# A graph network's merged stage: project the next group in the steps that attend to this one

## The chip, the cores and the metric

The kernel runs on one core of one Trainium2 chip. A core has a TensorE (PE, matmuls into PSUM), a VectorE (DVE), a ScalarE (ACT), a GpSimd (POOL) and a SyncE (SP, which here only issues DMAs). Each engine works through its own list of instructions in order and waits on semaphores for the others. The metric is the device time of one execution in microseconds; less is better.

## The reference

Two layers over 32768 nodes of 256 numbers and 524288 edges. Cut to what matters:

```python
h = relu(layernorm(x))                      # layer 0: attention within 128 nodes
Q, K, V = h @ Wq + bq, h @ Wk + bk, h @ Wv + bv     # 256 blocks, 8 heads of 32
scores = Q @ K.T / sqrt(32)                 # block 0 also adds a bias made of its edges
x = x + softmax(scores) @ V @ Wo + bo
h = relu(layernorm(x))                      # layer 1: one step of a gated graph network
h = (h - mean) * rsqrt(var + EPS) * gamma + beta    # over all nodes
a_in  = segment_sum((h @ W_in + b_in)[src] * iw, dst)
a_out = segment_sum((h @ W_out + b_out)[dst] * ow, src)
x = x + gated_update(h, [a_in, a_out] @ W_x2i + b_x2i, h @ W_h2h)
```

## The kernel before

The program has these stages in order: sort and count the edges and write tables (to about 950 us), attention of the first group, the merged stage (to about 9970 us), the sums over edges (to about 17100 us), and the gated update.

**Groups.** The attention is cut into 64 groups of 512 nodes, four blocks `b` of 128 each. `group(g)` (L719) gives the whole work of one group as a table from a step number to functions: `@at(t)` files a function under step `t`. Its parts, with their steps: load x into `xg` on ACT's queue (L744, step 0), add the bias row to it on POOL into `xb` (L748, step 3), layer norm (`row_stats`, `std`, reciprocal, `xn`: steps 2 to 8), transposes into `hT` (L739, L779: 6 to 10), queries and keys for the two halves `m` of the heads (L789, L795: 11 to 18; copied out at L799 and L808/L810), values (L820: 19 to 23). Then for each block `b`, from step B = 17 + 11 b: for each half `m`, scores (L837, at B + 4 m), their maximum (L845), exps on ACT (L851, two to a step), transposes of the exps (L857, from B + 3 and B + 7), their copy (L863/L865); then the product with the values (L873, B + 10 and 11), division (L880), transpose (L739, B + 13), output matmul (L895), sum with `xb` and statistics (L899, B + 16). After blocks 2 and 3: the root (`std`, L734), norm (L922), transposes (L739) and copies of the new rows, and their writes to memory. The last step is 71.

Queries lie in `qT`; keys in `kbd`, a tile with zeros between the heads; there is one set of each. The matmuls of a group write three PSUM banks, `mm`, `pt` and `sc`, one buffer each: a bank's next user waits until the one before is copied out.

**The merged stage.** `spread(k, lo, hi)` works for each of three parts of the edges in rounds of CI = 64 steps, 68 rounds in all. Each step handles a set of 128 edges, in a chain of operations that stand some steps apart (`steps`, L1115):

```python
steps = ((0, fetch), (4, spread_lanes), (6, select), (8, rank), (8, product), (8, place), (9, scale), (9, scatter))
```

`fetch` loads 128 rows `hb` (SP, ring of 10 buffers); `rank` is three bf16 matmuls into `R` (PE, two banks); `product` a float32 matmul into `mp` (PE, two buffers); `place` reads `R` (DVE, `jk`); `scale` copies `mp` into a message (ACT); `scatter` sends four messages each fourth step by an indirect DMA (POOL). `window` and `derive` prepare the next round's tables from step 10 and 24 on.

`turns` (L1117) writes the loop: a body of four rounds (`UG`) or of one, in which the steps are written out by hand in order for PE, DVE, ACT and SP (`manual_schedule`; POOL isn't in it). Within a step come the edge operations first, then the group's functions of that step. A round that carries a group adds the table of `group(g)` to its steps (L1130 to 1133); what lies past step 63 falls into the next round's first steps or, at the end of a body, into eight steps that only drain. At the end of a body all engines meet, and the loop starts empty.

The edges read rows that the groups write, so the groups must run ahead: the first group is done by `alone` (L950) before the stage, and a loop at L960 does more if a count made from the tables says so. 63 of the 68 rounds carry a group, in 21 loop bodies, 14 of four rounds and 7 of one; the last five rounds carry none.

Of the kernel before, what the change touches and what calls it, by code (L numbers as in the profile page):

```python
# [11 lines left out]
F32 = mybir.dt.float32  # L12
# [487 lines left out]
def gnn_kernel(ctx, tc, x, src, dst, edge_attr, edge_type, w_in_e, w_out_e,  # L500
# [186 lines left out]
    with ExitStack() as c1:  # L687
# [10 lines left out]
        kbd = ap.tile([P, KC, GB, HC, P], F32, name="kbd")  # L698
        nc.gpsimd.memset(kbd, 0.0)
# [14 lines left out]
        hT, qT, h1T = (ap.tile([P, KC, GN], F32, name=n) for n in ("hT", "qT", "h1T"))  # L714
# [4 lines left out]
        def group(g, bias=None):  # L719
# [3 lines left out]
            def at(t):  # L723
                def put(f):
                    todo.setdefault(t, []).append(f)
                return put

            def row_stats(i, b, rows):
                st = ab.tile([P, 6], F32, name="st")
                nc.vector.bn_stats(st, rows)  # L730
                nc.vector.bn_aggr(mv[i][:, b], st)

            def std(i, bs):
                nc.scalar.activation(rstd[i][:, bs], mv[i][:, bs, 1], AF.Sqrt, bias=eps)  # L734

            def transposed(name, rows):
                tp = a_ps.tile([P, KC, P], F32, name=name)
                for k in range(KC):
                    nc.tensor.transpose(tp[:, k], rows[:, k * P:(k + 1) * P], ident)  # L739
                return tp  # L740

            @at(0)
            def _():
                nc.scalar.dma_start(xg, x_g[g])  # L744

            @at(3)
            def _():
                nc.gpsimd.tensor_add(xb, xg, bo_b[:, None, :].to_broadcast([P, GB, D]))  # L748

            for b in range(GB):  # L750
# [3 lines left out]
                @at(2 + b // 2)  # L754
                def _(b=b):
                    row_stats(0, b, xg[:, b])

                if b == 0:
                    @at(4)
                    def _():  # L760
                        std(0, slice(0, GB))

                    @at(5)
                    def _():
                        nc.vector.reciprocal(rstd[0], rstd[0])

                @at(5 + b)
# [5 lines left out]
                @at(6 + b)  # L773
                def _(b=b, row=row):
                    row["tp"] = transposed("pt" if b % 2 else "mm", row["xn"])

                @at(7 + b)
                def _(row=row, cols=cols):
                    nc.scalar.activation(hT[:, :, cols], row["tp"], AF.Relu)  # L779

            for m in range(KC):
                ps = {}
                mc = slice(m * P, (m + 1) * P)
                for k in range(KC):
                    @at(11 + 4 * m + k)
                    def _(m=m, k=k, ps=ps, mc=mc):
                        if k == 0:
                            ps["q"] = a_ps.tile([P, GN], F32, name="mm")
                        nc.tensor.matmul(ps["q"], wq[:, k, mc], hT[:, k], start=(k == 0), stop=(k == KC - 1))  # L789

                    @at(13 + 4 * m + k)
                    def _(m=m, k=k, ps=ps, mc=mc):
                        if k == 0:
                            ps["k"] = a_ps.tile([P, GN], F32, name="pt")
                        nc.tensor.matmul(ps["k"], wk[:, k, mc], hT[:, k], start=(k == 0), stop=(k == KC - 1))  # L795

                @at(13 + 4 * m)
# [3 lines left out]
                for j in range(HC):  # L801
                    @at(15 + 4 * m + j // 2)
# [9 lines left out]
            for b in range(0, GB, 2):  # L812
                ps = {}
                for i in range(2):
                    @at(19 + 3 * (b // 2) + i)
                    def _(b=b, i=i, ps=ps):
                        if i == 0:
                            ps["v"] = a_ps.tile([P, 2, D], F32, name="mm")
# [4 lines left out]
                @at(21 + 3 * (b // 2))  # L823
                def _(b=b, ps=ps):
                    nc.scalar.copy(vg[:, b:b + 2, :, 0:DH], ps["v"].rearrange("p b (h d) -> p b h d", d=DH))

            for b in range(GB):
                B = 17 + 11 * b
# [88 lines left out]
                for n, u in enumerate(range(bs.start, bs.stop)):  # L917
                    h = {}

                    @at(B + 18 + n)  # L920
# [3 lines left out]
                    @at(B + 19 + n)  # L924
                    def _(u=u, h=h):
                        h["tp"] = transposed("pt" if u == 1 else "sc", h1g[:, u])
# [497 lines left out]
```

## Time and profile before

| | us |
|---|---|
| median of seven runs | 19516.0 (19507.79 to 19544.12) |
| the profiled execution | 19532.19 |
| its span, first to last instruction | 19530.4 |
| PE busy | 14804.8 (76%) |
| DVE busy | 10004.3 (51%) |
| POOL busy | 9288.9 (48%) |
| ACT busy | 6698.5 (34%) |
| granted PE clock, mean | 0.885 |

Busy times are of the whole span and mix four stages, so they don't say what sets a stage's time. "A <- B" in a line means that A stood idle until B ended, with the total, the number of times and the longest. "issue" as a releaser means that nothing visible was waited for, and "remote" a release from outside the core's engines. The granted clock is the share of PE's full clock that it was given.

### The profile page before, as it was taken

The numbers are of one execution on the slowest core, as the hardware profiler recorded it, in microseconds if no ns is written. First come the engines' busy times: TensorE is split into PE (matmuls) and PEld (weight loads), VectorE is DVE, ScalarE is ACT, GpSimd is POOL, SyncE is SP. The second block draws the span as 40 slices with busy tenths as digits, with TensorE's granted clock in tenths as the row PEclk, the third lists the DMA queues.
The fourth block names the chain that finished last, engine by engine and source line by source line (L and its number), as shares of the span: only waits on it lengthen the run. The fifth ranks groups of instructions, "written<-read, shape, count | busy, mean of one in ns | idle before, by whom it ended". The sixth has DMA issues, their size and how long they took to land. (4 is left out here: it accounts for less than half of the span.)

```text
span 19530.4 us, 292322 instructions
## 1 busy us (share of the span) xinstructions
PE 14804.8 (76%) x71746; PEld 10613.8 (54%) x71746; DVE 10004.3 (51%) x33799; ACT 6698.5 (34%) x16865; POOL 9288.9 (48%) x9307
## 2 busy tenths in 40 slices
PE   2078777787777777777668787778787778788889
PEld 2055555555555455555456666666666666653334
DVE  8666666566666566665444444444444444432222
ACT  0044444444444444444223333333333333320000
POOL 0045545455554455544555555555555555532222
PEclk6598889888888898988779999899998998999999
DMA  2044444444444444444446666677766677673332
GB/s 64 7 146 151 147 144 148 135 147 148 147 145 143 138 129 145 147 142 140 134 143 196 193 197 196 183 199 198 196 197 184 193 197 199 195 151 111 108 111 96
DMA packets 1829625, 2975.41 MB, mean 152 GB/s; under 512 B 299498, under 2 KB 1288135, under 8 KB 1827670
## 3 DMA queue, kind: packets, MB, share of 16 engines
q1 hardware_dynamic: 1169398, 1550.90, 26.3%
q0 software_dynamic: 430768, 1160.40, 20.3%
q10 hardware_dynamic: 227888, 246.51, 4.0%
q8 instruction: 577, 9.45, 0.2%
q14 instruction: 994, 8.14, 0.1%
HBM read 2123.63 MB, written 1248.64 MB: 173 GB/s over the span
## 5 line engine op out<-in xcount | busy, mean ns | idle before, releaser
L1108 POOL DMA_INDIRECT msg_d<-msg,pi x4352 | 4287.3, 985 | 3962.6 <-issue 1719.8
L1230 POOL DMA_INDIRECT rows<-h_d,ixc x3584 | 3398.8, 948 | 2323.6 <-issue 744.0
L1099 DVE SCALAR_TENSOR_TENSOR jk<-iota,edc,R 128x256 f32<-128x256 bf16 x4352 | 2077.1, 478 | 3064.6 <-PE R L1079 1443.8
L1091 ACT ACTIVATE msg<-mp,edc 128x256 f32<-128x256 f32 x4352 | 2048.6, 476 | 3614.2 <-PE mp L1075 1893.6
L1265 ACT ACTIVATE selo<-lane_row,sl 128x128 f32<-128x128 f32 x5040 | 1661.3, 391 | 4696.3 <-DVE sl L1262 1596.9
L1244 PE MATMUL ps_i<-rows,sel 128*128 128x257 f32 x8960 | 2637.0, 415 | 811.2 <-DVE acc L1248 415.8
L1272 PE MATMUL ps_o<-m,selo 128*128 128x257 f32 x10080 | 2754.0, 413 | 587.1 <-ACT selo L1266 265.0
L1075 PE MATMUL mp<-hb,selT 128*128 128x256 f32 x8704 | 2875.5, 415 | 131.2 <-issue 74.0
L1272 PEld LDWEIGHTS ps_o<-m,selo 128*128 128x128 f32 x10080 | 1969.3, 205 | 981.9 <-issue 289.4
L1244 PEld LDWEIGHTS ps_i<-rows,sel 128*128 128x128 f32 x8960 | 1641.1, 207 | 1106.6 <-DVE acc L1248 476.7
L1237 DVE TENSOR_SCALAR sel<-lane_row,ed 128x128 f32<-128x128 f32 x4480 | 1393.6, 360 | 1006.1 <-PE idle L1245 378.4
L1079 PE MATMUL R<-oh,ones_b 128*128 128x256 bf16 x4352 | 1275.4, 293 | 500.9 <-DVE jk L1099 268.5
L1276 DVE SCALAR_TENSOR_TENSOR acc<-acc,blk,ps_o 128x257 f32<-128x257 f32 x1680 | 806.2, 480 | 1553.8 <-PE ps_o L1272 569.9
L1075 PEld LDWEIGHTS mp<-hb,selT 128*128 128x128 f32 x8704 | 1453.0, 210 | 268.2 <-issue 99.9
L1071 DVE TENSOR_SCALAR oh<-iota,edc 128x256 bf16<-128x256 bf16 x4352 | 1356.9, 312 | 4.1
L1079 PE MATMUL R<-oh,tri 128*128 128x256 bf16 x4352 | 1269.9, 292 | 0.0
L1079 PE MATMUL R<-oh,triu 128*128 128x256 bf16 x4352 | 1266.8, 292 | 2.6 <-DVE jk L1099 2.5
L1248 DVE SCALAR_TENSOR_TENSOR acc<-acc,blk,ps_i 128x257 f32<-128x257 f32 x2240 | 1071.1, 478 | 249.8 <-issue 69.6
L1230 POOL DMA_INDIRECT rows<-h_d,ixh x896 | 849.7, 948 | 649.9 <-issue 252.6
L1262 DVE TENSOR_SCALAR sl<-m,blk 128x3 f32<-128x3 f32 x1680 | 419.6, 250 | 1248.3 <-DMA m<-msg_d 1043.5
L1266 ACT ACTIVATE selo<-selo,one 128x384 f32<-128x384 f32 x1680 | 1031.3, 614 | 52.2
L1245 PE MATMUL idle<-lane_row,sel 128*128 128x128 f32 x4480 | 869.6, 283 | 166.8 <-DVE sel L1237 136.4
(366 smaller groups left out, 20442.0 us busy)
## 6 DMA issues: line engine op xcount, KB each, us to landing
m<-msg_d SPq DMA_DIRECT2D x1680, 396.0 KB
hb<-h_d SPq DMA_DIRECT2D x4352, 128.0 KB
sin_d<-acc SPq DMA_DIRECT2D x2240, 128.5 KB
sout_d<-acc SPq DMA_DIRECT2D x1680, 128.5 KB
msg_d<-msg,pi POOLq DMA_INDIRECT x4352
more<-sout_d ACTq DMA_DIRECT2D x128, 514.0 KB
rows<-h_d,ixc POOLq DMA_INDIRECT x3584
a<-sin_d ACTq DMA_DIRECT2D x64, 514.0 KB
```

The costliest lines, as they stand in the source:

```text
L1071: nc.vector.tensor_scalar(oh, cn["iota1"], c["ed"][:, 0, q:q + 1], None, op0=ALU.is_equal)
L1075: nc.tensor.matmul(mp, turn["sel", i // 4][:, q % 4], turn.pop(("hb", i)), start=True, stop=True)
L1079: nc.tensor.matmul(R[to % 2], cn[what], oh, start=False, stop=False, skip_group_check=True)
L1091: nc.scalar.activation(msg[:, q % 4, 0:D], turn.pop(("mp", i)), AF.Copy, scale=c["ed"][:, 1, q:q + 1])
L1099: nc.vector.scalar_tensor_tensor(jk, cn["iota1"], c["ed"][:, 0, q:q + 1], R[i % 2], op0=ALU.is_equal, op1=ALU.mult, accum_out=c["pf"][:, q ...
L1108: s = nc.gpsimd.indirect_dma_start(out=msg_d[k][:], out_offset=bass.IndirectOffsetOnAxis(ap=c["pi"][:, j:j + 1], axis=0), in_=msgs[i // 4 ...
L1230: nc.gpsimd.indirect_dma_start(out=rows[(2 * i + r) % NR][:, 0:D], out_offset=None, in_=h1_d[:], in_offset=bass.IndirectOffsetOnAxis(ap=(i ...
L1237: nc.vector.tensor_scalar(sel[:, r], cn["lane_row"], c["ed"][:, 0, r, i:i + 1], c["ed"][:, 1, r, i:i + 1], op0=ALU.is_equal, op1=ALU.mult)
L1244: nc.tensor.matmul(ps, sel[:, r], rows[(2 * i + r) % NR], start=(r == 0), stop=(r == 1))
L1248: nc.vector.scalar_tensor_tensor(acc[0][i % NA], acc[0][(i - 1) % NA], c["blk"][:, 0, i:i + 1], c.pop(("t_ps", i)), op0=ALU.mult, op1=ALU.add)
L1265: nc.scalar.activation(sel[:, r], cn["lane_row"], AF.Abs, bias=sl[:, r:r + 1])
L1272: nc.tensor.matmul(ps, sel[:, r], m[:, r, 0:FW], start=(r == 0), stop=(r == T3 // P - 1))
```

## The change

`group` is split in two. `project(g, qT, kbd)` loads, norms and projects a group; `attend(g, qT, kbd)` does the rest. There are two sets of queries and keys. A round attends to group `g` from one set while, in the same 64 steps, it loads and projects group `g + 1` into the other.

```diff
-        kbd = ap.tile([P, KC, GB, HC, P], F32, name="kbd")
-        nc.gpsimd.memset(kbd, 0.0)
+        kbds = [ap.tile([P, KC, GB, HC, P], F32, name=f"kbd{i}") for i in range(2)]
+        for t in kbds:
+            nc.gpsimd.memset(t, 0.0)
...
-        hT, qT, h1T = (ap.tile([P, KC, GN], F32, name=n) for n in ("hT", "qT", "h1T"))
+        hT, h1T, *qTs = (ap.tile([P, KC, GN], F32, name=n) for n in ("hT", "h1T", "qT0", "qT1"))
...
-        def group(g, bias=None):
+        def project(g, qT, kbd):
...
-            @at(0)
+            @at(5)
             def _():
-                nc.scalar.dma_start(xg, x_g[g])
+                nc.sync.dma_start(xg, x_g[g], bounds_check="skip_entire_dma")
...
-                @at(2 + b // 2)
+                @at(9 + b // 2)
                 def _(b=b):
                     row_stats(0, b, xg[:, b])
...
-                @at(5 + b)
+                @at(17 + 2 * b)
                 def _(b=b, row=row):
                     xn = row["xn"] = ab.tile([P, D], F32, name="xn")
...
-                @at(6 + b)
-                def _(b=b, row=row):
-                    row["tp"] = transposed("pt" if b % 2 else "mm", row["xn"])
-                @at(7 + b)
+                @at(18 + 2 * b)
+                def _(row=row):
+                    row["tp"] = transposed("mm", row["xn"])
+                @at(19 + 2 * b)
                 def _(row=row, cols=cols):
                     nc.scalar.activation(hT[:, :, cols], row["tp"], AF.Relu)
+            @at(11)
+            def _():
+                std(0, slice(0, GB))
+            @at(12)
+            def _():
+                nc.vector.reciprocal(rstd[0], rstd[0])
...
+                bank = ("pt", "mm")[m]
                 for k in range(KC):
-                    @at(11 + 4 * m + k)
+                    @at(26 + 7 * m + k)
-                    @at(13 + 4 * m + k)
+                    @at(29 + 7 * m + k)
-                @at(13 + 4 * m)
+                @at(28 + 7 * m)
-                    @at(15 + 4 * m + j // 2)
+                    @at(31 + 7 * m + j // 2)
...
-            for b in range(0, GB, 2):
+            for b, t, bank in ((0, 41, "pt"), (2, 59, "sc")):
...
+            @at(63)
+            def _():
+                nc.gpsimd.tensor_add(xb, xg, bo_b[:, None, :].to_broadcast([P, GB, D]))
+            return todo
+        def attend(g, qT, kbd, bias=None):
+            todo, at = steps_of()
             for b in range(GB):
-                B = 17 + 11 * b
+                B = 1 + 15 * b
...
-                    @at(B + 18 + n)
+                    @at(B + 18 + 2 * n)
...
-                    @at(B + 19 + n)
+                    @at(B + 19 + 2 * n)
                     def _(u=u, h=h):
-                        h["tp"] = transposed("pt" if u == 1 else "sc", h1g[:, u])
+                        h["tp"] = transposed("mm", h1g[:, u])
-                    @at(B + 20 + n)
+                    @at(B + 20 + 2 * n)
...
-            alone(0, bias)
-        with tc.For_i(1, planned(4 * K, 1, NG), 1) as it:
-            alone(it)
+            emit(project(0, qTs[0], kbds[0]))
+            emit(attend(0, qTs[0], kbds[0], bias))
+        lead_n = planned(4 * K, 1, NG)
+        with tc.For_i(1, lead_n, 1) as it:
+            emit(project(it, qTs[0], kbds[0]))
+            emit(attend(it, qTs[0], kbds[0]))
+        emit(project(lead_n.with_bounds(min_val=0, max_val=NG - 1), qTs[0], kbds[0]))
...
-                                        for u, fs in group((it + groups + r).with_bounds(min_val=0, max_val=NG - 1)).items():
-                                            assert u < CI + last
-                                            todo.setdefault(t + u, []).extend(fs)
+                                        now, then = r % 2, (r + 1) % 2
+                                        g = lambda i: (it + groups + (r + i)).with_bounds(min_val=0, max_val=NG - 1)
+                                        for work in (attend(g(0), qTs[now], kbds[now]), project(g(1), qTs[then], kbds[then])):
+                                            for u, fs in work.items():
+                                                assert u < CI + last
+                                                todo.setdefault(t + u, []).extend(fs)
...
                         add("triu", n - 1, n - 1, turn)
+                        if groups is not None and nr % 2:
+                            nc.vector.tensor_copy(kbds[0], kbds[1])
+                            nc.scalar.copy(qTs[0], qTs[1])
```

In `attend`, a block's own steps relative to B are as before, but for the last three, which stand two steps apart for each row block in place of one. Its blocks now start at steps 1, 16, 31 and 46, and its last step is 67. A body of one round ends with a copy of the second set into the first, since the next body starts from the first. The group after the last doesn't exist: its load is skipped by the bounds check, and its projection works on what lies there.

## The prediction

> **What bounds the kernel now.** I read the share of each stage first, then who the TensorE (PE) waits for inside one stage, then ScalarE's instructions in order, then the end of a loop body. The change touches only the merged stage, from about 1030 to 9970 us of the span of 19530.4 us. The windows view of that stage, two rounds that carry a group and then two late rounds that carry none (us, busy us and count of PE, weight loads, DVE, ACT, POOL, granted clock, DMA share, GB/s):
>
> ```profile
> 5089.50:5219.50 130.00, 109.94 (x568) 76.57 (x566) 79.52 (x296) 57.87 (x149) 65.65 (x66) 0.86 0.45 146
> 5220.00:5347.00 127.00, 103.06 (x572) 70.90 (x571) 81.48 (x299) 57.21 (x147) 66.13 (x66) 0.89 0.47 149
> 9347.00:9463.00 116.00, 77.36 (x384) 48.13 (x383) 57.56 (x239) 31.68 (x82) 60.64 (x62) 0.78 0.44 139
> 9474.00:9588.00 114.00, 76.61 (x379) 48.46 (x379) 56.73 (x235) 31.98 (x82) 61.73 (x63) 0.77 0.44 141
> ```
>
> In a group round PE is busy 107 of 128.5 us, DVE 80, POOL 66, ACT 58: PE sets the pace, by its work in order and by what it waits for. A round without a group still takes 114 to 116 us; that is a floor under everything below. The waits of PE over the first two windows (us in total, times, longest):
>
> ```profile
> PE R L1079 <- DVE jk L1099: 10.2, 8, 3.2
> PE pt L857 <- DVE oh L1071: 4.8, 2, 2.4
> PE pt L857 <- ACT F L1038: 4.4, 2, 2.4
> PE pt L795 <- issue: 4.2, 2, 3.0
> PE mm L739 <- DVE o L880: 4.1, 3, 1.5
> PE sc L739 <- ACT h1g L922: 3.7, 2, 1.8
> PE pt L857 <- ACT kbd L808: 2.6, 1, 2.6
> PE mp L1075 <- ACT msg L1091: 1.9, 2, 1.0
> PE pt L857 <- ACT msg L1091: 1.9, 1, 1.9
> PE pt L857 <- DVE PT L865: 1.5, 1, 1.5
> PE pt L857 <- issue: 1.5, 1, 1.5
> ```
>
> With 3.4 us of smaller lines they make 44.2 us, which is what the windows leave (257 - 213.0). Per round: A, the ranks that wait for DVE (R), 5.1; B, the transposes of the softmax (pt L857), 8.35; C, the keys' matmuls (pt L795), 2.1; D, the transposes of the attention's output, 2.05; E, those of the new rows (sc), 1.85; F, the products that wait for ACT (mp), 0.95; the rest 1.7. Sum 22.1.
>
> Counting the rank matmuls places each wait at a program step. B falls on steps 20 (2.07 on average of 27 like rounds: bank pt is still read by the copies into kbd, and exps follow a table load), 35 (2.33: the ACT copies F of steps 35 and 36 stand among the exps), 46 (1.53: nothing but the chain scores, maximum, exps) and 57 (2.34: two table loads). C is step 17. ScalarE near step 56, in order of time:
>
> ```profile
> 5313.50 1.28 ACT L734 ACT_TABLE_LOAD   x1
> 5314.80 0.30 ACT L734 ACTIVATE rstd<-mv,eps 128x3 f32<-128x3 f32 x1
> 5315.11 1.28 ACT L851 ACT_TABLE_LOAD   x1
> 5316.40 0.62 ACT L851 ACTIVATE pr<-sc,nm 128x128 f32<-128x128 f32 x2
> ```
>
> A change from Exp to Sqrt and back costs 1.28 us twice. There are four such loads in a round. The last view is PE at the end of a loop body (5473 to 5500 us):
>
> ```profile
> PE bc L1064 <- DVE dlbc L1052: 12.2, 1, 12.2
> PE mm L739 <- DVE xn L770: 6.4, 1, 6.4
> ```
>
> The first wait is drain and refill of the loop; rounds without a group show it too, with 12.2 us. The second is the new group's own start: load x, statistics, root, norm, first transposes, with nothing else to do.
>
> **The change, part by part (us per group round unless said).**
> *Waits of PE.* No work of a round is taken away but the order, so I price the seven groups of waits again.
> A, 5.1 to 4.0: the statistics of x stood two steps behind its load and waited for it (68.3 us between 1200 and 9200 us, 60 rounds, 1.1 each); now four steps. Against that, step 32 holds on DVE a sum and its statistics (0.42 + 0.43 + 0.18), a maximum (0.67) and two key copies (0.74 each over 31 and 32), which are queued ahead of place (jk), and PE's ranks wait for jk. Ends 2.0 and 6.5.
> B, 8.35 to 7.1: the key copies leave bank pt a step before its next user (29, 30 written, 31, 32 copied, 34 used) and F no longer meets exps. But three of the four second halves (steps 8, 23, 53) have little PE work between scores and transposes: 3 x 1.5, the row of step 46; step 38 has the q and k matmuls before it, 0. Steps 4 and 19 stand behind a table load, whose 1.28 can run while ACT waits for the maximum: 0.9 each. Step 49 keeps two loads: 0.8. Sum 7.1, ends 5 and 10.
> C, 2.1 to 0 (q and k share a bank with a copy a step between; at most 1). D and E keep their distance of one step: 2.05 and 1.85, ends 3.0 and 5.0 for both. The rest 1.7, ends 1 and 2.
> F, 0.95 to 1.5: the table loads rise from four to six (Exp at 3, Sqrt at 11, Exp at 18, Sqrt and Exp at 48, Sqrt at 63), and msg copies are queued behind each; products wait as soon as a copy is two late, the ring of mp. Ends 0.95 and 2.5.
> Sum 18.2, a gain of 3.9; the good ends sum to 11.95 (gain 10.1), the bad ones to 27.0 (loss 4.9).
> *Clock.* The granted clock is 0.86 and 0.89, so up to 0.125 x 128.5 = 16 of PE's time is lost to it. Work that lies more evenly leaves fewer dull stretches; I take 2, an eighth, between -2 and 8. The sum is 5.9 per round; 68 rounds, 63 with a group: 372 us.
> *Loop ends.* 21 loop bodies carry groups (14 of four rounds, 7 of one). The 6.4 us for x, norm and transposes go: x was loaded a round ago. In their place PE waits for the first exps: maximum 0.67, table load 1.28, two exps 0.74 = 2.7, of which some lies beside the refill; I take 2.5, ends 0 and 5. Gain 3.9 x 21 = 82, between 29 and 134.
> *A group projected before the stage.* One more projection runs alone. The first group's took from its load at 949.75 to its values at 979.8, 30 us; about half can lie beside the first attention: +15, ends 5 and 30. The last round projects a group that doesn't exist: its load is skipped, its matmuls are those of any round.
> *Copies.* Seven one-round bodies copy a set of keys (4096 numbers a row) on DVE and queries on ACT. DVE sits idle 12.1 us before each new body, waiting for the scatters; so 0. Without that cover a 512-number copy of 0.68 us says 5.5 each, 38 in all. The second fill of kbd (3.51 us on POOL) lies in POOL's idle 7 us before xb: 0.
> *The load on SP.* It leaves ACT's queue (0.40 us of issue) for SP's, where it stands ahead of the fetches of hb from step 5 on and waits until POOL has added xb (2.35 us, step 63). SP's own time goes mostly to waiting for PE (1492 us for products alone between 1200 and 9200), and ten hb buffers leave eight steps, 15 us: 0; if POOL were a whole row of eight scatters (10 us) behind, the rest of that slack would still hold. POOL's add no longer waits for x (189 us in 60 rounds); its cover was that POOL is no bound.
> Sum: 19532.2 (span 19530.4 and 1.8 around it) - 372 - 82 + 15 = 19093. The profiled execution is 16 above the median of 19516, so 19080.
>
> The page "ScalarE: Activation LUTs" of the Trainium skill (What ACT_TABLE_LOAD costs; Rules for kernel authors) says to do all of one table set before switching, and gives about 2.66 us to a switch, 1.28 for the load and the rest for a drain. That speaks against this change. The rows above show 1.28 and then the root at once, no drain. By the page two more switches would be 5.3 us of ACT per round, 335 in all, by the row 162; added to the forecast in full, that is 19415 by the page and 19240 by the row.
>
> **The rivals.**
> 1. *Slower: six table loads in the open.* At steps 4, 19 and 49 PE meets exps right behind a load, at 11, 48 and 63 the msg copies stand behind one. If each of the first three costs the 2.3 of step 57, each of the others its 1.28, and the three unfilled chains 1.5, then B + F is 15.3 in place of 8.6, the sum 24.9, and with a clock that loses 1 us each round is 3.8 longer: 239 - 82 + 15 = +172, 19690. It decides where B + F passes 13.3: 22.1 + 67/63 = 23.2 for the sum, without help of the clock. For it: 57's row. Against it: at steps 31, 42 and 53 the first halves wait 0.1, so a chain of a step each mostly holds.
> 2. *The rounds stay as they are.* Steps without group work are not free to run ahead: in the late rounds DVE stands until POOL has written a row of eight scatters.
>
> ```profile
> 9537.39 0.98 POOL L1108 DMA_INDIRECT msg_d<-msg,pi  x1 [0.30 <-issue]
> 9538.45 0.48 DVE L1099 SCALAR_TENSOR_TENSOR jk<-iota,edc,R 128x256 f32<-128x256 bf16 x1 [5.61 <-remote]
> ```
>
> What PE wins in one step it may wait in the next, and only the ends of the loops are left: 19532 - 82 + 15 = 19465, 19450. Against it: 128.5 is far from 114.
> 3. *Rounds at the floor.* If the even spread also keeps the clock up, rounds fall to 114: 14.5 x 63 = 914, with 82 and 15, 18550 and by the median 18535. Against it: DVE's and ACT's chains keep their lengths.
> That the change doesn't do what it says would show as projections that still wait for their own x; the load's place a round ahead excludes most of that.
>
> **How the numbers follow.** Forecast 0.50 (its own range 18800 to 19330, from gains of 2.5 to 10 per round); rival 3 0.12; rival 2 0.20, of which 0.07 within 0.2%; rival 1 0.18. 0.2%, 39 us, is about what a measurement of this kernel tells from no change (the seven runs spread over 36). Faster 0.50 + 0.12 + 0.13 = 0.75, same 0.07, slower 0.18. The range from 18700 to 19640 leaves out some 0.07 of rival 3 below and 0.12 of rival 1 above.
>
> **What would show it.** Over two group rounds: pt L795 gone from PE's waits (the keys' line), pt L857 near 14 us, R near 8, table loads 12; rounds of 122 to 123 us in place of 128.5; no wait for xn at a loop's start, but one for exps of 2 to 3 us; clock 0.88 to 0.92. The prediction is wrong if the transposes' waits pass 20 us in two rounds, if SP holds hb back (products waiting for a load), or if the stage ends where it did with waits only moved to R.

## The result, and the profile after

| | before | after |
|---|---|---|
| median, us | 19525.94 (37 runs, 19478.29 to 19586.16) | 19589.58 (15 runs, 19564.99 to 19629.53) |
| ratio | | 1.0032, 95% interval 1.0025 to 1.0040 |
| span of the profiled execution | 19530.4 | 19588.1 |
| first `jk` of the merged stage | 1032.0 | 1062.3 |
| first to last `jk` | 8931.6 | 8975.0 |
| what follows | 9566.8 | 9550.8 |
| four-round body, mean of 14 | 522.4 | 522.8 |
| one-round body, mean of 7 | 143.2 | 147.4 |

The change makes the kernel 0.3% slower; the forecast was 2.2% faster. The 57.7 us between the two spans (one profiled execution of each kernel) are 30.3 of a later start of the stage, 43.4 of the stage itself, and -16.0 behind it, where nothing was changed. Of the stage's part, 29 us lie in the one-round bodies (7 x 4.2), some 5 in the four-round ones, 4 in four of the rounds without a group; the rest lies in the last round.

The windows view of the same two group rounds and two late rounds as before (columns as there):

```profile
5145.00:5270.00 125.00, 101.25 (x573) 68.25 (x571) 80.88 (x300) 60.57 (x152) 66.18 (x67) 0.94 0.47 154
5270.00:5398.50 128.50, 103.64 (x571) 69.30 (x572) 81.50 (x300) 60.12 (x151) 67.01 (x67) 0.93 0.46 147
9414.50:9530.00 115.50, 75.66 (x378) 47.18 (x376) 55.66 (x232) 31.85 (x82) 61.65 (x63) 0.77 0.43 136
9541.00:9656.00 115.00, 77.76 (x376) 48.56 (x375) 56.48 (x232) 31.44 (x82) 61.64 (x63) 0.77 0.42 137
```

The two group rounds take 253.5 us in place of 257 and the late ones are as they were. PE's waits in the two group rounds:

```profile
PE R L1094 <- issue: 10.5, 4, 5.2
PE pt L869 <- issue: 7.5, 6, 2.6
PE R L1094 <- DVE jk L1114: 7.4, 5, 5.1
PE mp L1090 <- issue: 5.5, 5, 2.4
PE mp L1090 <- ACT msg L1106: 5.0, 7, 1.6
```

The keys' line is gone and the softmax transposes (`pt`) fall from 16.7 us to 8.3. What was taken from them stands at `R` and `mp`, the edge work: ranks, which need DVE's `jk` (10.2 to 17.9), and products, which need ACT's copies (1.9 to 12.9; smaller lines counted in). One such place in the order of time, first POOL, then DVE, ACT and PE (start, duration, in brackets the idle time before):

```profile
5671.65 0.93 POOL L1011 DMA_INDIRECT win<-rec_d,wix  x1 [0.30 <-issue]
5673.11 1.00 POOL L1123 DMA_INDIRECT msg_d<-msg,pi  x1 [0.52 <-issue]
...
5677.00 0.98 POOL L1123 DMA_INDIRECT msg_d<-msg,pi  x1 [0.30 <-issue]
5679.55 0.48 DVE L1114 SCALAR_TENSOR_TENSOR jk<-iota,edc,R 128x256 f32<-128x256 bf16 x1 [6.92 <-remote]
5679.59 0.47 ACT L1106 ACTIVATE msg<-mp,edc 128x256 f32<-128x256 f32 x1 [5.36 <-remote]
5680.09 0.37 PE L1094 MATMUL R<-oh,ones_b 128*128 128x256 bf16 x1 [5.11 <-DVE jk L1114]
```

From 5666.49 to 5677.98 POOL sends nine indirect DMAs in a row: four scatters, the `win` of the next round's window, four scatters. The rank that `jk` needs was on PE at 5673.9 and the product that `msg` needs at 5674.3 (their starts). Both engines stand until 1.6 us after the row's end, and PE with them. I call this *standing*: the time between the end of what `jk` (or `msg`) needs, or of its engine's instruction before, and its start.

What is late here comes from PE. In the trace's record of semaphores this `jk` waits for one alone, the one that PE raises. It shows no rise between 5673.73 and 5679.52, though three matmuls that raise it end in that time (5673.87, 5674.19, 5674.98), and then five within 0.23 us. SP's next load of `hb`, which waits for it too, also starts only at 5679.58. So "remote" in these lines doesn't mean a release from outside the core; it means one that lies near no instruction's end. A matmul's end in the profile is modelled, so the record doesn't tell whether the matmul or only its signal was late.

DVE's waits over the whole stage, before and then after:

```profile
DVE jk L1099 <- PE R L1079: 1443.5, 1389, 4.7
DVE jk L1099 <- remote: 424.3, 124, 6.4
```
```profile
DVE jk L1114 <- remote: 935.9, 237, 7.8
DVE jk L1114 <- PE R L1094: 893.3, 824, 4.4
```

Added up over the group rounds, DVE's standing is 1250 us before and 1497 after, ACT's 1177 and 1396 (the two overlap). POOL's rows of eight or more indirect DMAs (gaps under 0.6 us) rise from 79 to 140. How PE's signal goes with these rows can be counted. In the group rounds of before, its next rise comes more than 1 us late for none of the 2924 matmuls that raise it and end outside a row, and for 16% of those that end at a row's first DMA, 16% at the second, 32% at the third, 42% at the fourth and 56% at the fifth.

### The profile page after: what moved, and what is told of

It reads as the page before. It is cut to its first block, busy times and chain, and to the rows that moved or that the text cites. A ratio compares the mean times of both kernels' runs of the same rounds, so it can differ in the third digit from the quotient of the medians.

```text
span 19588.1 us, 292930 instructions
## 1 busy us (share of the span) xinstructions
PE 14918.1 (76%) x71786; PEld 10568.7 (54%) x71786; DVE 10026.4 (51%) x33823; ACT 6878.0 (35%) x17011; POOL 9327.7 (48%) x9309
## 5 line engine op out<-in xcount | busy, mean ns | idle before, releaser
L1090 PE MATMUL mp<-hb,selT 128*128 128x256 f32 x8704 | 2924.6, 421 | 311.8 <-ACT msg L1106 145.6
L1094 PEld LDWEIGHTS <-triu 128*128 128x128 bf16 x4352 | 447.1, 103 | 1199.6 <-issue 1055.0
```

The source lines that it names most:

```text
L1090: nc.tensor.matmul(mp, turn["sel", i // 4][:, q % 4], turn.pop(("hb", i)), start=True, stop=True)
L1094: nc.tensor.matmul(R[to % 2], cn[what], oh, start=False, stop=False, skip_group_check=True)
```

## The experiments

Theory P says that POOL's rows of indirect DMAs hold DVE and ACT and so eat the gain. Its rivals are T, that the two more table loads per round cost it, and S, that the load moved to SP or the work moved on DVE comes late.

The runs fell on chips of two kinds, and a comparison holds on one chip only: on some the kernel before takes 17517 to 17522 us (here *A*), on the others 19504 to 19628 (*B*, and the result is of this kind). Every ratio is to the kernel before on the same chip.

| run | chip | us, median | ratio, 95% interval |
|---|---|---|---|
| e1 after, one scatter a step | A | 17458.98 | 0.9963 (0.9951, 0.9975) |
| e2 before, one scatter a step | A | 17669.40 | 1.0090 (1.0075, 1.0106) |
| e3 after, first root on DVE | A | 17305.10 | 0.9880 (0.9862, 0.9898) |
| e4 after, no projection ahead | A | 17321.99 | 0.9893 (0.9877, 0.9910) |
| e5 after | A | 17347.19 | 0.9897 (0.9881, 0.9914) |
| e6 before (one run) | A | 17487.29 | |
| e7 after, no copies | A | 17342.31 | 0.9897 (0.9880, 0.9913) |
| e8 after, all roots on DVE | A | 17530.28 | 1.0009 (0.9998, 1.0020) |
| e9 as e1 | B | 19455.46 | 0.9906 (0.9884, 0.9927) |
| e10 after, one root per round | B | 19670.94 | 1.0022 (1.0011, 1.0033) |
| e11 e10, projection beside the first attention | B | 19638.23 | 1.0004 (0.9994, 1.0014) |
| e12 after, scatters four steps long | A | 17350.51 | 0.9906 (0.9889, 0.9922) |
| e13 before, the same | A | 17527.84 | 1.0004 (0.9994, 1.0013) |
| e14 after | A | 17356.50 | 0.9912 (0.9895, 0.9928) |
| e15 e12, projection beside the first attention | A | 17364.31 | 0.9914 (0.9898, 0.9931) |
| e16 as e12 | B | 19465.70 | 0.9977 (0.9965, 0.9989) |
| e17 as e13 | B | 19510.21 | 0.9997 (0.9988, 1.0007) |
| e18 after | B | 19448.96 | 0.9972 (0.9962, 0.9982) |

**The scatters apart (e1, e2, e9).** Each set gets a place tile of its own, and its scatter goes out at its own step:

```diff
-                if q % 4 == 3:
-                    c["pi"] = ip.tile([P, 4], I32, name="pi")
-                    nc.vector.tensor_add(c["pi"], c["pf"], c["ed"][:, 3, q - 3:q + 1])
+                turn["pi", i] = ip.tile([P, 1], I32, name=f"pi{q % 4}")
+                nc.vector.tensor_add(turn["pi", i], c["pf"][:, q % 4:q % 4 + 1], c["ed"][:, 3, q:q + 1])
...
-                if q % 4 == 3:
-                    for j in range(4):
+                if True:
+                    for j in (q % 4,):
```

> Theory P (POOL): what PE won in the changed order is taken back because DVE and ACT stand while POOL writes rows of four and eight indirect DMAs back to back. Here each set's scatter goes out in its own step in place of four each fourth step. P expects that no rows of eight are left in steady rounds, that place's standing with its ranks done (1722 us in the changed kernel) falls by more than half, that four-round bodies fall from 523 to 470-500 us, and a time of 18700 to 19200. Theory T (six ACT table loads hold ScalarE and PE) expects no change: 19560 to 19620, since the loads stay. Rival S (SP or DVE is the late engine): three more small DVE sums per four steps make it slower, 19620 to 19750.

> The same edit in the kernel before. P expects a gain too, smaller than in the changed kernel, since PE's own waits (8.2 us for the softmax's transposes per round) stay: 18900 to 19350, and the order of the two kernels turned round: the changed one ahead by 100 to 300 us. T expects 19500 to 19550 and the changed kernel still 0.3% behind.

Both became slower than their originals. e2 lies 148 us above the kernel before. e1 lies 63 below it, where the change without this edit lies 170 below (e5, on another chip A): some 107 lost. The traces told why neither could gain: there is nothing to be gained here. DVE's waits over the stage in e5, the changed kernel on a chip A:

```profile
DVE jk L1114 <- PE R L1094: 1588.2, 1501, 3.1
DVE rowc L1067 <- PEq L1135: 353.2, 19, 35.5
DVE nm L857 <- PE sc L849: 83.3, 39, 2.9
```

There is no line with "remote"; `jk` starts when its rank is done. POOL's rows are not shorter there (214 of eight or more in e5, 145 in e6) and a scatter takes the same 990 ns; yet DVE's standing in the group rounds sums to 73 us (e5) and 88 (e6), where the result's traces have 1497 and 1250. So e1 and e2 only price the edit itself, three more small DVE operations in four steps among it.

> The changed kernel with one scatter a step in place of four each fourth step, once more, for the case that the kernel before takes about 19520 us again, which is where the standing behind POOL's rows was seen. There theory P expects 19000 to 19400, below the changed kernel's 1.003 of before; if the standing does not come from rows of scatters (rival: it comes from the chip, whatever the rows), 1.003 to 1.012. Where the kernel before takes about 17520, it is a repetition: 0.996.

On a chip B the same kernel as e1 gives 19455 us, 0.9906: more than the 19000 to 19400 I expected, and yet below each reading of the unedited change there (1.0032 in the result, 0.9972 in e18). Rows of eight or more fall to 1, DVE's standing in group rounds to 792 us and ACT's to 827; PE's wait for `R` falls from 8.30 to 4.40 per round. What cost some 107 us on a chip A brings time here: the rows do hold DVE and ACT on this kind of chip. The changed kernel itself did not run on the chip of e9. Its nearest relatives there are e10 and e11 below (1.0022 and 1.0004), which keep the four scatters together: e9 takes 215 and 183 us less than they, and 201 of the 206 us between the spans of e9 and e10 lie in the merged stage. Standing isn't gone in e9, only about half of it.

**The change on both kinds of chip (e5, e6, e14, e18).** No edit.

> The changed kernel as it is. In the four runs before, the kernel before took 17522 us where it took 19526 in the result, and in their traces DVE's jk starts within 0.1 us of the rank it waits for, while in the result's two traces it stands up to 7 us behind POOL's rows of scatters (1468 us in all before, 1722 after). Theory P (the gain of the change is eaten by that standing): where the standing is absent the change pays, some 1% (17300 to 17380 beside 17522); where the kernel before takes 19520 again, the standing is there and the ratio is 1.003 again. Theory T (two more table loads per round, 2 x 1.28 us x 64 = 164 us, cost what the change wins): the ratio is 1.000 to 1.004 on either.

> The kernel before, for a profile of it beside the changed kernel's on one chip. Theory P, where it takes about 17520: sum of jk's standing near 0, the group rounds of four-round bodies some 2 to 3 us longer than those of the changed kernel; where it takes 19520: standing near 1470 us and rounds of equal length.

> The changed kernel as it is, beside the others on one chip. Where before takes about 19600: 1.001 to 1.005, as in the result; where it takes 17520: 0.988 to 0.991, as in e5.

> The changed kernel as it is on the chip of e16 and e17: 1.001 to 1.005 where before takes about 19600, 0.990 where it takes 17520.

Where nothing stands, the change pays 1.0% (e5) and 0.9% (e14). Where there is standing, it is 1.0032 once and 0.9972 once. Two group rounds and two late ones of e5:

```profile
4646.00:4759.00 113.00, 99.08 (x571) 68.04 (x570) 81.81 (x300) 59.55 (x151) 66.12 (x66) 0.94 0.55 175
4759.00:4868.50 109.50, 98.09 (x573) 67.49 (x574) 81.65 (x301) 60.09 (x152) 66.48 (x67) 0.95 0.53 170
8393.00:8476.00 83.00, 56.29 (x378) 40.33 (x376) 54.26 (x232) 32.30 (x82) 61.13 (x63) 0.87 0.59 189
8487.00:8572.00 85.00, 57.01 (x378) 40.70 (x376) 54.47 (x232) 32.29 (x82) 62.26 (x63) 0.84 0.58 187
```

The engines do the same counts of work; a late round takes 84 us in place of 115. My floor of 114 was this kind of chip's own.

Theory P has a ledger. DVE's standing in the group rounds, and the medians:

| | standing before | after | growth | gain of the change |
|---|---|---|---|---|
| A (e6, e5) | 88 | 73 | -15 | 17516.71 - 17347.19 = 169.5 |
| B (e17, e18) | 1266 | 1395 | 129 | 19504.14 - 19448.96 = 55.2 |
| B (result) | 1250 | 1497 | 247 | 19525.94 - 19589.58 = -63.6 |

The gain without standing, less the growth, would be 169.5 - 129 = 40 and 169.5 - 247 = -78; measured 55 and -64. (e17 stands in for the kernel before on its chip: it took 0.9997 of it.) Rows of eight or more are 95 in e17 and 155 in e18, as 79 and 140 in the result. By this ledger the sign of the change is the difference of two things of like size. That is arithmetic over three pairs of traces, not a proof for each pair, and some of its agreement may be luck: in the middle rounds of the table further down, PE's waits apart from standing fall by some 5 us on B and by 1.1 on A, so A's gain isn't simply B's without standing. Nor do the rows' numbers alone tell the standing (155 rows and 1395 us in e18, 140 and 1497 in the result).

**An edit without effect (e12, e13, e16, e17).** The four scatters were filed under four following steps, with their places still worked out together:

```diff
-                if q % 4 == 3:
-                    for j in range(4):
+                for m in range(i - 3, i - 2 if i < turn["n"] - 1 else i + 1):
+                    if m >= 0:
```

> The changed kernel with its four scatters sent one a step over the four steps after they are due, the places still worked out four at a time on DVE: no operation is added, only POOL's rows are taken apart. Theory P, where the kernel before takes about 19600: as e9 or better, 0.985 to 0.992 of before. Rival C (e1 and e9 differ from the changed kernel on the chip's account, not by the rows): 1.000 to 1.005. Where the kernel before takes about 17520: 0.988 to 0.992, as the changed kernel, if e1's loss there (0.9963 beside 0.9897) came from its extra operations on DVE; 0.995 to 0.998 if it came from the rows being apart.

> The same edit in the kernel before. Theory P, where before takes about 19600: the standing (1468 us in its trace, beside 1722 in the changed kernel's) is partly gone here too; if the change's gain was only eaten by the standing, this kernel gains less than the changed one does, 0.990 to 1.000, and the changed kernel with the edit stays 0.5 to 1% below it. If both gain alike, the standing doesn't explain the sign. Where before takes 17520: 0.998 to 1.003.

> e12 once more, for a chip on which the kernel before takes about 19600 us. Theory P there: 0.985 to 0.992 of before, as e9 or better. Rival C (not the rows): 1.000 to 1.005. Where before takes 17520: 0.990 again, which tells nothing new.

> e13 once more, for such a chip. If the change's gain was eaten by POOL's rows and nothing else, this edit gives the kernel before less than it gives the changed one: 0.990 to 1.000, above e16 by 0.5 to 1%. If it gives both the same, the rows cost both alike and the sign has another cause.

e12 equals e14 on one chip and e16 equals e18 on another, within their intervals. The trace says why it tests nothing: POOL is not among the engines with a written order, so filing a scatter under a later step doesn't delay it. POOL sends it as soon as places and messages are there, and those still come in fours: e16 has 151 rows of eight or more, e18 155. In e9 each place is ready at its own step, and that spaced the rows. My expectations for these four runs were wrong on that account, and the question whether the kernel before would gain as much on B by shorter rows was not answered: e2's edit ran on A only.

**Table loads (e3, e8, e10).** e3 works the projection's root out on DVE in one operation, which is close to the root only for variances near 1, as x has here; the kernel has four table loads a round in place of six:

```diff
-            @at(11)
-            def _():
-                std(0, slice(0, GB))
-            @at(12)
-            def _():
-                nc.vector.reciprocal(rstd[0], rstd[0])
+            @at(11)
+            def _():
+                nc.vector.tensor_scalar(rstd[0], mv[0][:, :, 1], -0.5, 1.5, op0=ALU.mult, op1=ALU.add)
```

> In the changed kernel the root of the projected group's variance is left out: DVE takes 1.5 - 0.5 v in one operation, so two of the six table loads of a round go (steps 11 and 18). T expects 63 x 2.6 us less, 19400 to 19460, and by the bottom of it half of that. P expects little, 19550 to 19600: the freed time shows up as longer standing behind POOL.

Its gain over the kernel before on its chip is 217 us, e5's on its own 170: 47 us for 2 x 64 loads of 1.28 us, 164 us of ACT. Some seven tenths of their time lay under other work (the edit also saves DVE a small operation).

In e8 every root of the merged stage is worked out on DVE, nine small operations a root:

```diff
-            nc.scalar.activation(rstd[i][:, bs], mv[i][:, bs, 1], AF.Sqrt, bias=eps)
+            nc.vector.tensor_scalar(v, mv[i][:, bs, 1], 1e-5, None, op0=ALU.add)
+            nc.vector.tensor_scalar(s, v.bitcast(I32), 1, None, op0=ALU.arith_shift_right)
+            nc.vector.tensor_scalar(y.bitcast(I32), s, -1.0, float(0x5f3759df), op0=ALU.mult, op1=ALU.add)
+            for _ in range(2):
+                nc.vector.scalar_tensor_tensor(t, y, -0.5, y, op0=ALU.mult, op1=ALU.mult)
+                nc.vector.tensor_mul(t, t, v)
+                nc.vector.scalar_tensor_tensor(y, t, 1.5, y, op0=ALU.add, op1=ALU.mult)
```

> The changed kernel with every root of the merged stage worked out on DVE (an integer first guess and two Newton steps, nine small operations), so that ScalarE changes its table no more: six loads per round become at most none. Theory T: all of 6 x 1.28 us lay in the open in part; e3, which took two of six away, was 0.988 of the kernel before; if T holds the other four bring as much each, 0.975 to 0.98. Theory P: the loads of steps 48 and 49 alone are in PE's way (PE waits 2.8 us at step 49), so 100 to 200 us below the changed kernel, and nothing where POOL's rows hold DVE.

All loads are gone from the rounds and the kernel is 183 us slower than e5. PE's waits in two group rounds of e5, then of e8:

```profile
PE mp L1090 <- ACT msg L1106: 5.4, 5, 1.8
PE pt L869 <- ACT pr L863: 4.7, 6, 1.9
PE mm L741 <- ACT h1g L934: 4.0, 2, 3.2
PE mm L741 <- DVE xn L763: 3.8, 4, 1.3
```
```profile
PE mm L751 <- ACT h1g L943: 11.9, 4, 5.5
PE mp L1099 <- ACT msg L1115: 5.2, 4, 1.8
PE mm L751 <- DVE xn L773: 2.9, 2, 1.6
PE R L1103 <- DVE jk L1123: 2.7, 4, 1.5
```

The exps' wait falls (`pt` 4.7 to 1.8 in e8), but the chain of nine dependent operations makes the norms (`h1g`) late by more. Table loads are not what eats the change, and they are cheaper than taking them all away in this manner.

e10 takes one root for all four blocks at step 63 and norms them one step apart, four loads a round:

```diff
-                if b < GB - 2:
+                if b < GB - 1:
                     continue
-                bs = slice(0, b + 1) if b < GB - 1 else slice(b, b + 1)
+                bs = slice(0, GB)
...
-                    @at(B + 18 + 2 * n)
+                    @at(B + 18 + n)
```

> The changed kernel with one root for all four blocks at step 63 in place of two (step 48 for three blocks, step 63 for the last): four table loads per round in place of six, no root in the middle of the exps, the norms and their transposes at steps 64 to 68 one step apart. If the loads at steps 48 and 49 are what PE waits for at step 49 (1.9 us per round there in the changed kernel's trace, 2.5 in the result's): 60 to 120 us below the changed kernel, 0.984 to 0.987 of before where that takes 17520. If the norms' chain at the round's end only takes the wait over, as in e8 (transposes of the new rows 1.8 to 5.5): no gain or a loss of up to 100 us.

The wait at step 49 falls as expected (`pt` there 2.5 to 0.7 per round), but the waits at `R` are 9.7 us per round beside 8.3 in the result, and those of the new rows' transposes 2.8 beside 1.8: in all 24.3 beside 22.8. The ratio is 1.0022, on a chip without a run of the change beside it. No gain is seen; how it would do on a chip A is open.

**The projection ahead of the stage, and the copies (e4, e7, e11, e15).** e4 leaves the line out that projects a group before the stage, so that the first merged round attends with the first group's queries and keys. e7 leaves the copies out, so that the round behind each works with old queries and keys. e11 and e15 emit that projection in the steps of the first attention, by the same merging of tables as in the rounds, with a copy behind it (the three parts below in that order):

```diff
-        emit(project(lead_n.with_bounds(min_val=0, max_val=NG - 1), qTs[0], kbds[0]))
...
-                        if groups is not None and nr % 2:
-                            nc.vector.tensor_copy(kbds[0], kbds[1])
-                            nc.scalar.copy(qTs[0], qTs[1])
...
-            emit(attend(0, qTs[0], kbds[0], bias))
+            both = attend(0, qTs[0], kbds[0], bias)
+            for u, fs in project(1, qTs[1], kbds[1]).items():
+                both.setdefault(u, []).extend(fs)
+            emit(both)
```

> The projection that stands alone ahead of the merged stage is left out (the first merged round attends with the first group's queries and keys). Both theories: the first rank of the stage starts 1062 us into the profiled span in the changed kernel, 1032 before; without it 1030 to 1036, so 19555 to 19565. If the 30 us are the loop that stands between or the second fill of the keys' tile, it stays above 1045 and 19575.

> The changed kernel without the copy of the second set of queries and keys into the first at the end of the seven one-round bodies; the round after each attends with old queries and keys. The prediction put the copies at 0 (hidden in the drain), 38 us in all if not; in the result's traces the seven one-round bodies grew by 4.2 us each. If the copies are in the open: 25 to 40 us shorter than the changed kernel. If they are hidden: within 10 us of it.

> e10, and the projection of the second group is emitted in the steps of the first group's attention, before the stage, with a copy of its queries and keys, in place of alone behind it. e4, which leaves that projection out, started the stage 24 us earlier (1045.3 in place of 1069.6). If the projection can lie beside the first attention: 10 to 20 us below e10; if the two wait for each other's banks: as e10, within 5 us.

> e12 with the second group's projection emitted in the steps of the first attention, before the stage. e11 lies 33 us below e10 by the medians with intervals that almost meet, and its stage starts only 4 us earlier (1060.5 beside 1064.4); e4 allows 24. So 4 to 24 us below e12, and the best of all where rows hold DVE.

The first `jk` comes at 1045.3 in e4 and at 1068.0 in e1 and e3, on the same chip; that is 23 us of the 30 that the prediction counted for a projection, so most of it lies in the open. Merging it into the first attention brings 4 to 5 us of that at the stage's start (1060.5 for 1064.4 on one chip, 1064.5 for 1069.8 on another). e15 is no faster than e12; e11 is 33 below e10 by medians, more than its start explains, and that rest stays open. The copies cost 1.5 us each at six of the seven ends (from the last `jk` of a one-round body to the next body's first: 29.0 in e5, 27.5 in e7) and 5.4 at the seventh, behind which no group follows (19.9 and 14.5): 14 in all, too little for the medians to tell.

## Why the prediction was wrong, point by point

PE's idle time per group round ahead of each kind of matmul, from the same 28 rounds of each trace (the second and third rounds of the fourteen four-round bodies), with the windows' sums under it:

| wait | forecast | B before | B after | A before (e6) | A after (e5) |
|---|---|---|---|---|---|
| A, ranks for `jk` | 5.1 to 4.0 | 6.70 | 8.30 | 2.45 | 1.17 |
| B, softmax transposes | 8.35 to 7.1 | 8.24 | 4.92 | 7.61 | 3.28 |
| C, keys | 2.1 to 0 | 1.60 | 0 | 0.02 | 0 |
| D, output transposes | 2.05 | 2.33 | 0.46 | 0.16 | 0.39 |
| E, new rows' transposes | 1.85 | 2.19 | 1.82 | 2.82 | 1.80 |
| F, products for `msg` | 0.95 to 1.5 | 1.32 | 4.43 | 0.00 | 2.80 |
| transposes of `xn` | in the rest | 0.65 | 1.97 | 0.47 | 1.89 |
| the rest | 1.7 | 0.78 | 0.89 | 0.57 | 1.67 |
| sum | 22.1 to 18.2 | 23.81 | 22.79 | 14.10 | 13.00 |
| PE busy | | 103.78 | 103.66 | 98.48 | 97.44 |
| round | 5.9 shorter | 127.67 | 126.47 | 112.72 | 110.44 |

*Waits of PE, A: the step that failed.* The prediction read 5.1 us of waits for `jk` as DVE's queue (statistics, maxima, key copies) and priced moves in that queue. Of the 6.7 us that the 28 rounds of before show, 4.6 are ranks whose `jk` had itself stood (over 0.3 us); in the two windows that it read these are 4.7 of 10.2 us. I quoted a `jk` that stood in the second rival and still let A fall to 4.0. It rose to 8.3, above even its bad end of 6.5. The part without standing fell from 2.1 to 0.8, about as priced, and on chips A, where nothing else is in it, from 2.45 to 1.17. The part with standing rose from 4.6 to 7.5, and that of the products (F) from 0.5 to 1.6. These 3.9 us a round eat most of what the other waits gave. DVE's standing in these rounds moved more than it grew (20.9 us a round before, 22.5 after): `jk` of step 12 stood 0.01 us on average before and 5.0 after, and the rank of step 14, which needs it, accounts for 3.8 of the 8.3. The prediction's own last sign of being wrong, a stage that ends where it did with waits moved to `R`, is what came.

*B and C: right in kind, too small.* With a step between each copy and its bank's next user, C vanished, and B fell by 3.3 where I gave 1.25. D fell by 1.9 as well on B, unforeseen. Together these save 6.8 us a round on a chip B. The even spread was priced too cautiously, and what was given back at `R` and `mp` was not priced at all.

*F: the wrong cause.* I priced F by table loads. ACT and PE at step 34 of e5, without any load:

```profile
4690.83 0.68 ACT L810 ACTIVATE kbd<-pt,bk_c 32x512 f32<-32x512 f32 x1 [3.20 <-DVE kbd L812]
4691.53 0.47 ACT L1106 ACTIVATE msg<-mp,edc 128x256 f32<-128x256 f32 x1
4692.06 0.70 PE L1090 MATMUL mp<-hb,selT 128*128 128x256 f32 x2 [1.78 <-ACT msg L1106]
```

ACT's key copy waits 3.2 us for DVE's, the message is queued behind it, and the product behind the message. The keys' move to steps 31 to 39 put this pair among the messages; 2.54 of F's 2.80 on A fall on steps 34 and 41. On B products whose `msg` had stood add 1.6.

*The rest: `xn` missed.* At step 17 the norm of x stands on DVE behind a block's sum, its statistics and a maximum; PE's transposes at 18 and 22 wait 1.9 us. I had the contents of step 32 added up and not those of step 17.

*Clock: no help on B.* The granted clock of these rounds goes from 0.904 to 0.912, and PE's busy time by 0.12 us, for a forecast of 2. On A it is 0.939 to 0.961 and 1.04 us.

*Loop ends: gained, then given back.* PE in the place answering to the one shown of before (PEq is PE's own sequencer):

```profile
PE sc L849 <- PEq L1135: 10.9, 1, 10.9
PE R L1094 <- issue: 2.2, 1, 2.2
PE R L1094 <- DVE jk L1114: 0.9, 1, 0.9
PE pt L869 <- ACT pr L863: 0.7, 1, 0.7
```

The 6.4 us for `xn` are gone. From the last `jk` of a four-round body to the next body's first, 23.21 us became 19.94: 3.3 gained, 3.9 forecast. But over twenty sets to either side of the end, 93.75 became 94.40. What was won at the end was waited for in the steps around it. A body as a whole is 0.4 us longer though its two middle rounds are 2.4 shorter together; the 2.1 us beyond those twenty sets lie in its first and last round and were not taken apart. On A the same stretch went from 86.95 to 80.26, more than forecast. This is the second rival's sentence ("what PE wins in one step it may wait in the next"), which I applied to the rounds and not to the loops' ends.

*Projection ahead:* 30.3 us in place of 15, the far end of its range; on A 23 to 28. *Copies:* 1.5 us each in place of 0, and 5.4 at one end. The one-round bodies lost 4.2 each on B and gained 0.6 on A; of the 4.2 the copies explain 1.5, the rest was not taken apart. *Load on SP:* PE's matmuls and weight loads wait 2.2 us for `hb` in the whole stage, as good as nothing, as forecast. The longer distance paid on B, where DVE's waits for `xg` fall from 72.0 us to 3.5 (5.8 in e18), the 1.1 a round that A's price counted on. On A x still arrives when DVE asks for it (71.8 us in e6, 66.4 in e5).

The slower rival (six table loads in the open) is not what happened: the loads did rise to 12 in two rounds, but B and F came to 9.35 us, where it needed 13.6 (its 13.3 is a slip: 23.2 less the 9.6 of the other terms). e3 puts a load at some 0.37 us (47 us / 128), below the 1.28 of the row and the 2.66 that the Trainium skill's page "ScalarE: Activation LUTs" (What ACT_TABLE_LOAD costs) gives to a switch; no run here shows its drain. The second rival named the mechanism, at 0.20, with a price that kept the loops' gain and left out a row's growth. Even without standing the forecast was too high: 169.5 us on A, for 439 (372 + 82 - 15).

## What to carry to other kernels

Before you price a wait, ask whether its engine was late or its releaser: a `jk` that starts 5 us after its rank, just behind a row of POOL's DMAs, is not cured by moving DVE's work; a signal of PE's that comes late is not DVE's fault. Here work packed more evenly on PE went with a queue that nothing paces, POOL's, bunching up, and the gain was paid back there: look not only at how much an engine stands but at who waits for it just then. An edit to a queue without a written order changes nothing unless it changes when its inputs come; look at the rows in the trace first. And a change whose gain and loss are of one size has no sign of its own: 0.990, 0.997 and 1.003 are one kernel.

Best here on A is e3 (0.988), on B the one with scatters apart, e9 (0.9906), each against before; the two edits together were not run, nor a version of e9 without its added DVE operations.

## What the runs showed of the hardware

One and the same kernel takes 10 to 11% less on a chip A than on a B, with like durations of single instructions: in the stage a scatter's median is 983 ns on both (before and e6), a rank matmul's 273 and 273, a `jk`'s 480 and 479. Of the 2045 us between the spans of before on B and on A (e6), 1002 lie in the merged stage, where DVE's standing is 1468 us and 91 and the granted clock 0.882 and 0.910; 1052 lie behind it and were not taken apart. Four of the rounds without a group, loop ends included, take 508 us on B and 387 on A.

The standing takes in DVE and ACT alike (1497 and 1396 us after), and it goes with POOL's rows. In the group rounds of before, `jk` stands over 1 us in none of the 958 cases whose rank ends outside a row, in 4% of those at a row's first DMA, 15% at its second, 13% at its third and 26% at its fourth. On A the rows are longer and PE's signal is not late: its next rise lies over 1 us behind a matmul that raises it in 10 of 10956 cases in e5, and in 2047 of 10957 in the result. In e9, with the scatters apart, it still does in 2156 of 10956; so spacing the DMAs doesn't take the late signals away, it leaves DVE less often waiting for one (`jk` stands over 1 us 297 times in place of 489). (On B many rises are recorded together or not at all, so these counts are rough.)

The Trainium skill's page "Trainium Architecture — The Big Picture" (What this means for kernel authors) says that one engine doesn't block another unless a semaphore stands between them, and that on the engines' side of SBUF only the pair of ports that VectorE and GpSimd share contends. The traces of A agree. On B the engines that stand do wait on a semaphore, PE's, and ACT, no party to that pair, starts late at the same moment as DVE (5679.59 and 5679.55 above); so the ports alone don't explain it. What makes PE's signal late on B, and why some chips don't do it, no run here settles.
